# Two transformer layers with cross attention: cross keys in tiles of 512, 512, 450 and 127, the 450 first in a round, and small operations set between maxima

## The chip, the cores and the metric

The kernel runs on one core of a Trainium2 chip. The metric is the device time of one launch in microseconds, the median of several runs. TensorE (PE in the profile) multiplies matrices into PSUM, which has 8 banks of 128 partitions by 512 floats; VectorE (DVE), ScalarE (ACT) and GpSimd (POOL) do the rest; SyncE (SP, its queue SPq) issues nearly all the transfers (DMA).

## The reference

Two layers over x (4 sequences of 512 tokens, 320 wide) and a context (4 x 1601 tokens, 192 wide), all in float32. The part that the change touches is the attention, 20 heads of 16:

```
h1 = _ln(x, n1_g, n1_b)
x = _attn(h1, h1, q1, k1, v1, o1_w, o1_b, heads) + x
h2 = _ln(x, n2_g, n2_b)
x = _attn(h2, context, q2, k2, v2, o2_w, o2_b, heads) + x
...
sim = jnp.einsum('bhid,bhjd->bhij', q, k) * scale
a = jax.nn.softmax(sim, axis=-1)
out = jnp.einsum('bhij,bhjd->bhid', a, v)
```

A gated feed-forward layer follows in each of the two layers. The softmax is taken with the maximum of each row subtracted.

## The kernel before

**Units.** Attention is cut into units: one sequence and a group of 4 of the 20 heads. A layer has 20 self units (512 keys, 4 chunks of 128 keys) and 20 cross units (1601 keys, 13 chunks), then 4 feed-forward units. The four heads of a unit lie in four row groups of 32 partitions, so that matmuls of four heads can run side by side on PE.

**A round.** A unit's main loop takes one chunk of 128 keys a round (`main`). For each head `score` issues three matmuls of 512 columns into a bank named st: two of keys times queries (the queries are split in a high and a low part), and one that adds the rows nrows, the negated maxima. ACT takes the exponential out of st into pr. One round later `values` multiplies pr by the values into a bank named av, which ACT copies (vo) and POOL adds up.

**Maxima ahead.** The maxima must be known before a unit starts, so each round also computes scores of the next unit with queries on the partitions, only for their maxima: matmuls into banks named sps, reduced by DVE into pm (line 1083), one maximum for each query tile, head and key tile. `max_pairs` builds two queues for a unit, one for heads 2 and 3 and one for heads 0 and 1. An entry is a key tile of 512 of one query tile for both heads. Cross keys are cut into 512, 512, 512 and a rest of 65; the rest of all four query tiles shares one bank (66 columns each, reduced at line 1105). That makes 13 entries in each queue and 13 rounds in a cross unit. In a round the scores of heads 0 and 1 stand beside maxima of heads 2 and 3, then scores of 2 and 3 beside maxima of 0 and 1; `round_of` puts the passes of the four row groups into common slots, five in a round. `give` decides whether a round gets an entry, and whether whole further rounds of maxima are put in when the next unit is behind.

**End of a unit's maxima.** Two rounds before the end of a unit (`c == u.nch - 3`) `max_reduce` (line 1123, cross units only) takes the maximum over key tiles, and `max_end` makes a high part (1131), a low part (1134) and a transpose (1139), all on DVE, one behind the other. Four transfers on SPq (line 1147) carry the result into nrows; between cross units they are an errand that is issued at the end of the next round.

**Banks.** `bank` gives out the PSUM bank that is expected to be free first. The expectation is kept by `busy` and `written` from assumed durations. The same expectation decides in `taken` whether DVE or ACT copies the projections of values and keys.

Of the kernel before, what the change touches and what calls it, by code (L numbers as in the profile page):

```python
# [23 lines left out]
P = 128  # L24
# [24 lines left out]
AHEAD = 10  # L49
GAP = 3  # L50

PARTS = [(0, 2 * HG), (2 * HG, H)]
# [23 lines left out]
def kernel(ctx: ExitStack, tc: tile.TileContext, x, context, ws, out):  # L76
# [977 lines left out]
    def max_pairs(u):  # L1054

        full = u.nkeys // 512
        rest = u.nkeys - full * 512
        ns = full + (1 if rest else 0)
# [4 lines left out]
        def full_two(heads, t, s):  # L1063
            pss = []

            def product(e):
                for j, ps in zip(heads, pss):
                    nc.tensor.matmul(  # L1068
                        ps,
                        lhsT=u.q[j * SLOT : (j + 1) * SLOT, e, t * P : (t + 1) * P],  # L1070
                        rhs=u.kT[j * SLOT : (j + 1) * SLOT, u.k0 + s * 512 : u.k0 + (s + 1) * 512],
                        start=(e == 0),
                        stop=(e == 1),
                    )

            if ns == 1:
                to = u.nm[:, :, 0, t]
            else:
                to = u.pm[:, t, :, s]

            def reduce():
                for j, ps in zip(heads, pss):
                    nc.vector.tensor_reduce(to[:, j : j + 1], ps, AX.X, ALU.max)  # L1083
                    busy("dve", 0.6, ps)

            return heads, [lambda e=e: product(e) for e in range(2)], reduce, pss, lambda: pss.extend(bank("sps") for _ in heads)

        def rest_two(heads):
            pss = []
            w = rest + rest % 2  # L1090

            def product(t):
                for e in range(2):
                    for j, ps in zip(heads, pss):
                        nc.tensor.matmul(  # L1095
                            ps[:, t * w : (t + 1) * w],
                            lhsT=u.q[j * SLOT : (j + 1) * SLOT, e, t * P : (t + 1) * P],
                            rhs=u.kT[j * SLOT : (j + 1) * SLOT, full * 512 : full * 512 + w],
                            start=(e == 0),
                            stop=(e == 1),  # L1100
                        )

            def reduce():
                for j, ps in zip(heads, pss):
                    nc.vector.tensor_reduce(
                        u.pm[:, :, j, full], ps[:, : NQ * w].rearrange("p (t w) -> p t w", w=w)[:, :, :rest], AX.X, ALU.max,
                    )
# [4 lines left out]
        pairs = [  # L1112
            deque([lambda heads=heads, t=t, s=s: full_two(heads, t, s)] for s in range(full) for t in range(NQ))
            for heads in ((2, 3), (0, 1))
        ]
        if rest:
            for q, heads in zip(pairs, ((2, 3), (0, 1))):
                q.append([lambda heads=heads: rest_two(heads)])
        return pairs

    def max_reduce(u):
        if u.pm is not None:
            nc.vector.tensor_reduce(
                u.nm[:, :, 0, :].rearrange("p j t -> p t j"), u.pm, AX.X, ALU.max,
            )
            busy("dve", 0.25)

    def max_end(u):

        top, high, low = (u.nm[:, :, i, :] for i in range(3))  # L1130
        nc.vector.tensor_reduce(
            high.bitcast(F32R), top.rearrange("p j (t o) -> p j t o", o=1), AX.X, ALU.max, negate=True
        )
        nc.vector.tensor_reduce(
            low, u.nm[:, :, 0:2, :].rearrange("p j e t -> p j t e"), AX.X, ALU.add, negate=True
        )
        turned = two.tile([P, SLOT], F32, tag="turned", name="turned")

        nc.vector.transpose(turned.rearrange("p (j c) -> p j c", j=HG), u.nm[:, :, 1:3, :].rearrange("p j e t -> p j (e t)"))
        busy("dve", 0.6)  # L1140
        slots = u.rows.bitcast(F32).rearrange("(g s) n -> s g n", s=DH)[0].rearrange("g (t r) -> g t r", t=NQ)

        def rows():
            for i in range(P // SLOT):
                part = slice(i * SLOT, (i + 1) * SLOT)
                queue = (nc.sync, nc.scalar, nc.gpsimd, nc.sync)[i] if start["on"] else nc.sync
                queue.dma_start(out=slots[:, :, part], in_=turned[part, :])

        if u.cross and u.before.cross:
            u.rows_of = rows  # L1150
            errands.appendleft((clock["round"] + 1, yes, rows))
        else:
            rows()

# [132 lines left out]
    def main(u, give, nxt):  # L1287
# [62 lines left out]
        for c in range(u.nch):  # L1350
# [4 lines left out]
            else:  # L1355
                products = []
                for odd in range(2):
                    if odd:
                        tick()
                    pair, rounds = give(2 * c + odd)  # L1360
# [19 lines left out]
            if not last and c == u.nch - 3:  # L1380
                max_reduce(nxt)
                max_end(nxt)
# [52 lines left out]
    def ff_main(u, give, nxt):  # L1435
        done = 0

        def beside(room, n):
# [6 lines left out]
            if done == u.steps - 1 and nxt is not None and nxt.kind != "ff":  # L1445
                max_reduce(nxt)
                max_end(nxt)
            steps(True)
            for _ in range(n - 1):
# [149 lines left out]
    def giver(u):  # L1599
# [15 lines left out]
        def give(h, alone=False):  # L1615
# [21 lines left out]
            while owed >= 1.0 and any(left(v) for v in ahead) and not (alone and rounds and rest > -4):  # L1637
# [9 lines left out]
                at_once(v)  # L1647
                rounds.append([f for q in v.pairs if q for f in q.popleft()])
# [6 lines left out]
            return [], rounds  # L1655

# [24 lines left out]
    for chain in ("proj", "proj", "values", None):  # L1681
        round_of(first.pairs[0].popleft() + first.pairs[1].popleft())
        if chain:
# [3 lines left out]
    run("values")  # L1687
    max_reduce(first)
    max_end(first)
    loads.extend(load_x(2))  # L1690
    for fs in (load_out(0, "o1_w"), load_x(3), load_cross(0)):
# [3 lines left out]
    for _ in range(2):  # L1695
        round_of(second.pairs[0].popleft() + second.pairs[1].popleft())
        run("values")
# [51 lines left out]
```

## Time and profile before

| | |
|---|---|
| median of 3 runs | 2946.09 us (2944.18 to 2946.61) |
| span of the profiled execution | 2948.5 us |
| mean granted TensorE clock | 0.993 |
| instructions | 84388 |
| maxima of 512 keys into pm | 1920, mean 681 ns |
| maxima of the rests | 160, mean 425 ns |
| transposes at the end of a unit's maxima | 80, 16.9 us busy |

The profile is of one execution. Times in a timeline are microseconds from the span's start: start, duration, engine, line, instruction, what it writes and reads, and how many instructions of that kind are merged in the row; in brackets how long the engine had been idle and what released it. PEld is PE's weight load. The list of waits gives waiter, what it waited for, total us, number of times and the longest. Matmuls of different row groups overlap, so their durations do not add up.

### The profile page before, as it was taken

What the parts mean: (1) busy time and instruction counts of PE and PEld (TensorE: products, weight loads), DVE (VectorE), ACT (ScalarE), POOL (GpSimd) and SP (SyncE); (2) the same over time, 40 slices, a digit from 0 to 9 for tenths busy, and PEclk for the clock granted to TensorE, in tenths of its full rate; (3) what the DMA queues carried; (4) which work ended last, traced back from release to release, by engine and by line L of the source; (5) the groups of instructions that cost most, each with busy time, mean ns of one, the idle gap of its engine ahead of it and who ended that gap; (6) DMA issues with size and microseconds to landing.
All of it is one profiled execution on the core that took longest, in us unless ns stands there. A gap on an engine that the chain in (4) does not pass through costs nothing.

```text
span 2948.5 us, 84388 instructions
## 1 busy us (share of the span) xinstructions
PE 2871.7 (97%) x35018; PEld 1513.0 (51%) x35018; DVE 2060.2 (70%) x4031; ACT 1890.3 (64%) x3754; POOL 1287.7 (44%) x1409
## 2 busy tenths in 40 slices
PE   8999999999999999999999999999999999999999
PEld 4555555555555554355554555555555555544554
DVE  7777888888888878323258678888888888873221
ACT  3867677887877878501138676778778788783000
POOL 3556345545545545211225563455455464451110
PEclk8999999999999999999999999999999999999999
DMA  4444224232232112200113342222221121222000
GB/s 106 107 124 101 69 67 108 52 89 59 50 93 68 47 50 62 83 18 11 42 40 89 100 101 68 64 62 54 54 65 47 50 72 45 58 53 78 20 22 14
DMA packets 186543, 188.70 MB, mean 64 GB/s; under 512 B 69668, under 2 KB 137264, under 8 KB 186160
## 3 DMA queue, kind: packets, MB, share of 16 engines
q1 hardware_dynamic: 185368, 182.11, 24.4%
q8 instruction: 276, 4.52, 0.6%
q10 hardware_dynamic: 760, 1.18, 0.2%
q14 instruction: 107, 0.88, 0.1%
q0 software_dynamic: 32, 0.00, 0.0%
HBM read 55.76 MB, written 29.36 MB: 29 GB/s over the span
## 4 chain that ended last, share of the span: by engine, by line
PE 81%; DVE 13%; ACT 1%; DMA 1%; issue 1%; POOL 1%; SPq 1%; POOLq 0%; ACTq 0%; DVEq 0%
PE av L1326 22%; PE st L1300 16%; PE fps L1411 10%; DVE pm L1083 8%; PE sps L1068 6%; PE yps L1518 6%; PE vps L1029 5%; PE ops L1226 3%; PE kps L965 3%; PE qkps L900 3%; DVE nmax L1083 3%; PE fps L1471 2%; PE qps L941 2%; PE sps L1095 1%; ACT pr L1310 1%
## 5 line engine op out<-in xcount | busy, mean ns | idle before, releaser
L1310 ACT ACTIVATE pr<-st 128x512 f32<-128x512 f32 (+1 forms) x2720 | 1404.4, 604 | 399.8 <-PE st L1300 364.9
L1083 DVE TENSOR_REDUCE pm<-sps 128x1 f32<-128x512 f32 x1920 | 1188.0, 681 | 147.7 <-PE sps L1068 139.0
L1346 POOL TENSOR_TENSOR o<-o,vo 128x512 f32<-128x512 f32 x576 | 739.2, 1283 | 960.8 <-ACT vo L1345 937.5
L1068 PE MATMUL sps<-kT,q 32*128 32x512 f32 x4800 | 867.5, 430 | 10.6 <-DMA q<-low 3.4
L1300 PE MATMUL st<-q,kT 32*128 32x512 f32 (+1 forms) x5120 | 782.4, 420 | 2.2 <-ACT low L916 1.7
L1326 PE MATMUL av<-pr,vals 128*32 128x512 f32 (+1 forms) x5440 | 736.8, 607 | 45.5 <-ACT pr L1310 10.0
L1300 PEld LDWEIGHTS st<-q,kT 32*128 32x128 f32 (+1 forms) x5120 | 417.2, 180 | 290.4 <-issue 120.4
L1300 PE MATMUL st<-nrows,ones 32*128 32x512 f32 (+1 forms) x2720 | 539.1, 399 | 9.4 <-DMA nrows<-turned 9.4
L1068 PEld LDWEIGHTS sps<-kT,q 32*128 32x128 f32 x4800 | 425.6, 184 | 91.1 <-ACT pr L1310 13.4
L1083 DVE TENSOR_REDUCE nmax<-sps 128x1 f32<-128x512 f32 x640 | 396.3, 681 | 103.6 <-PE sps L1068 96.0
L1345 ACT COPY vo<-av 128x512 f32<-128x512 f32 x576 | 354.1, 615 | 23.9 <-PE av L1326 20.1
L1482 ACT ACTIVATE gl<-fps,b 128x512 f32<-128x512 f32 x80 | 54.6, 687 | 414.4 <-PE fps L1471 303.2
L1411 PE MATMUL fps<-hT,w 128*128 128x512 f32 x640 | 283.0, 597 | 0.0
L1326 PEld LDWEIGHTS av<-pr,vals 128*32 128x32 f32 (+1 forms) x5440 | 111.1, 108 | 320.4 <-DVE pm L1083 182.1
L1300 PEld LDWEIGHTS st<-nrows,ones 32*128 32x128 f32 (+1 forms) x2720 | 245.1, 180 | 34.4 <-issue 8.4
L1483 DVE SCALAR_TENSOR_TENSOR hid<-fps,b,gl 128x512 f32<-128x512 f32 x80 | 59.6, 748 | 241.1 <-ACT gl L1482 239.1
L1411 PEld LDWEIGHTS fps<-hT,w 128*128 128x128 f32 x640 | 119.3, 190 | 155.3 <-issue 152.1
L1518 PE MATMUL yps<-w,hid 128*128 128x320 f32 x640 | 176.3, 435 | 0.1
L1518 PEld LDWEIGHTS yps<-w,hid 128*128 128x128 f32 x640 | 120.4, 190 | 56.5 <-ACT gl L1482 4.5
L1226 PEld LDWEIGHTS ops<-wo,aT 112*32 112x32 f32 (+1 forms) x3072 | 97.9, 110 | 57.9 <-issue 41.2
L1226 PE MATMUL ops<-wo,aT 112*32 112x160 f32 (+1 forms) x3072 | 124.1, 300 | 0.7 <-POOL aT L1208 0.6
L517 POOL TENSOR_SCALAR root<-root 128x4 f32<-128x4 f32 x22 | 5.2, 237 | 263.9 <-DVE root L511 263.2
(91 smaller groups left out, 2493.1 us busy)
## 6 DMA issues: line engine op xcount, KB each, us to landing
kT<-stages SPq DMA_DIRECT2D x160, 200.2 KB
oway<-o SPq DMA_DIRECT2D x80, 256.0 KB
q<-high SPq DMA_DIRECT2D x160, 64.0 KB
q<-low SPq DMA_DIRECT2D x160, 64.0 KB
kT<-high SPq DMA_DIRECT2D x60, 128.0 KB
q<-high SPq DMA_DIRECT2D x60, 128.0 KB
kT<-low SPq DMA_DIRECT2D x57, 128.0 KB
aT<-oway SPq DMA_DIRECT2D x32, 224.0 KB
```

The source lines that it names most:

```text
L900: nc.tensor.matmul(ps[f : f + m, :w], lhsT=wqk[:n, k, f // GD, column : column + m], rhs=first.hT[:n, k, at : at + w], start=(k == 0), sto ...
L1029: nc.tensor.matmul(ps[f : f + m, :w], lhsT=u.kvT[:n, k, at + f : at + f + m], rhs=wv[:n, k, h0 * DH : h1 * DH], start=(k == 0), stop=(k == ...
L1068: nc.tensor.matmul(ps, lhsT=u.q[j * SLOT : (j + 1) * SLOT, e, t * P : (t + 1) * P], rhs=u.kT[j * SLOT : (j + 1) * SLOT, u.k0 + s * 512 : u ...
L1083: nc.vector.tensor_reduce(to[:, j : j + 1], ps, AX.X, ALU.max)
L1226: nc.tensor.matmul(ps[f : f + m, : D // 2], lhsT=aT[:n, k, f * NQ + t * SLOT : f * NQ + t * SLOT + m], rhs=wo[:n, k, cols], start=(k == 0) ...
L1300: nc.tensor.matmul(own[0][:r, :], lhsT=ones[rows, :r] if e == 2 else u.keys(rows, c), rhs=u.rows[rows, :] if e == 2 else u.q[rows, e, :], ...
L1310: nc.scalar.activation(p[:r], own[0][:r], AF.Exp)
L1326: nc.tensor.matmul(ps[j * SLOT : (j + 1) * SLOT, :], lhsT=columns_of[:r, head : head + SLOT], rhs=pr.pop((c, j))[:r, :], start=True, stop= ...
L1345: nc.scalar.copy(vo, ps)
L1346: nc.gpsimd.tensor_tensor(u.o, u.o, vo, ALU.add)
L1411: nc.tensor.matmul(ps, lhsT=w1[:, k, i * FF + c * P : i * FF + (c + 1) * P], rhs=natural(u.hT[:, k]), start=start, stop=stop,)
L1518: nc.tensor.matmul(ps[:, :D], lhsT=hid[c][:, t * P : (t + 1) * P], rhs=w2[:, c, :], start=(c == 0), stop=(c == NHC - 1),)
```

## The change

Cross keys are cut into 512, 512, 450 and 127. The number of entries stays 13 in each queue. A tile is now built for one head at a time (`one_tile`), and an entry joins two: in eight entries of each queue one tile of 450 of one head stands ahead of one of 512 of the other, in four both are 512, and the last holds the rests, now 4 x 127 keys of 128 columns. In the first eight entries those with a 450 alternate between the two queues. A round puts the half whose entry has a 450 first. The small operations that end a unit's maxima go into a list, and one of them is issued behind each maximum (`one_between`); what is left at the end of the round is issued there (`all_between`). The costs that `busy` is told follow the tile's width, and the rest's goes from 0.38 to 0.6.

```
+NARROW = 450
...
+        spans = [(at, min(512, u.nkeys - at)) for at in range(0, u.nkeys, 512)]
+        if u.cross:
+            spans = [(0, 512), (512, 512), (1024, NARROW), (1024 + NARROW, u.nkeys - 1024 - NARROW)]
...
+            def reduce():
+                nc.vector.tensor_reduce(to, own[0][:, :w], AX.X, ALU.max)
+                busy("dve", 0.065 + w * 0.00104, *own)
+                one_between()
...
-                    busy("dve", 0.38, ps)
+                    busy("dve", 0.6, ps)
+                    one_between()
...
+        for first, (a, b) in enumerate(((2, 3), (0, 1))):
+            wide = {j: deque((j, t, s) for s in range(2) for t in range(NQ)) for j in (a, b)}
+            slim = {j: deque((j, t, 2) for t in range(NQ)) for j in (a, b)}
...
+                if i == 12:
+                    q.append((False, [lambda a=a, b=b: rest_tiles((a, b))]))
+                elif i % 2 == first or i > 7:
+                    j, k = ((a, b), (b, a))[turn % 2]
+                    turn += 1
+                    q.append((True, entry(slim[j].popleft(), wide[k].popleft())))
+                else:
+                    q.append((False, entry(wide[a].popleft(), wide[b].popleft())))
...
+    def one_between():
+        if between:
+            between.popleft()()
...
+        between.extend(([over_spans] if u.pm is not None else []) + [leading, trailing, turn])
...
-                    products += [lambda j=j: score(c, j) for j in ((2, 3) if odd else (0, 1))] + pair
-                round_of(products)
+                    halves.append((not slim, [lambda j=j: score(c, j) for j in ((2, 3) if odd else (0, 1))] + pair))
+                round_of([f for _, half in sorted(halves, key=lambda h: h[0]) for f in half])
             u.scored = c + 1
 
             if extra and u.cross:
                 round_of(extra[0])
+            all_between()
             flush()
...
             if not last and c == u.nch - 3:
-                max_reduce(nxt)
                 max_end(nxt)
```

The first place is on PE, the last-but-one round of a cross unit: kT_135 and q_104 are that unit's keys and queries, kT_101 and q_103 those of the unit after the next, whose first maxima stand in this round. Before:

```order
L1300 MATMUL st<-q_104,kT_135 128x512 x2
L1068 MATMUL sps<-kT_101,q_103 128x512 x2
L1300 MATMUL st<-q_104,kT_135 128x512 x2
L1068 MATMUL sps<-kT_101,q_103 128x512 x2
L1300 MATMUL st<-nrows_97,ones 128x512 x2
L1300 MATMUL st<-q_104,kT_135 128x512 x4
L1068 MATMUL sps<-kT_101,q_103 128x512 x2
L1300 MATMUL st<-nrows_97,ones 128x512 x2
L1068 MATMUL sps<-kT_101,q_103 128x512 x2
```

And now:

```order
L1341 MATMUL st<-q_104,kT_135 128x512 x2
L1073 MATMUL sps<-kT_101,q_103 128x450
L1073 MATMUL sps<-kT_101,q_103 128x512
L1341 MATMUL st<-q_104,kT_135 128x512 x2
L1073 MATMUL sps<-kT_101,q_103 128x450
L1073 MATMUL sps<-kT_101,q_103 128x512
L1341 MATMUL st<-nrows_97,ones 128x512 x2
L1341 MATMUL st<-q_104,kT_135 128x512 x4
L1073 MATMUL sps<-kT_101,q_103 128x512 x2
L1341 MATMUL st<-nrows_97,ones 128x512 x2
L1073 MATMUL sps<-kT_101,q_103 128x512 x2
```

The number and place of the matmuls is the same; the first tile that is complete, and whose maximum DVE takes first, has 450 columns.

The second place is on DVE, the end of a cross unit's maxima: the rests (128x4), a further round of maxima, the small operations into nmax_95 and turned, and maxima of the unit after it. Before:

```order
L1105 TENSOR_REDUCE pm<-sps 128x4 x4
L1083 TENSOR_REDUCE pm<-sps 128x1 x4
L1123 TENSOR_REDUCE nmax_95<-pm 128x4x4
L1131 TENSOR_REDUCE nmax_95<-nmax_95 128x4x4
L1134 TENSOR_REDUCE nmax_95<-nmax_95 128x4x4
L1139 STREAM_TRANSPOSE turned<-nmax_95 128x32
L1083 TENSOR_REDUCE pm<-sps 128x1 x8
```

And now:

```order
L1109 TENSOR_REDUCE pm<-sps 128x4 x4
L1084 TENSOR_REDUCE pm<-sps 128x1 x5
L1160 TENSOR_REDUCE nmax_95<-pm 128x4x4
L1084 TENSOR_REDUCE pm<-sps 128x1
L1166 TENSOR_REDUCE nmax_95<-nmax_95 128x4x4
L1084 TENSOR_REDUCE pm<-sps 128x1
L1172 TENSOR_REDUCE nmax_95<-nmax_95 128x4x4
L1084 TENSOR_REDUCE pm<-sps 128x1
L1178 STREAM_TRANSPOSE turned<-nmax_95 128x32
L1084 TENSOR_REDUCE pm<-sps 128x1 x4
```

The transpose moved behind the fourth maximum of the next round. The four transfers of its result keep their place among SPq's instructions between cross units; in nine self units they moved behind one load of weights or inputs.

More of the change, by code (lines that the diff above doesn't have):

```diff
@@ L1116, in max_pairs, with entry @@
[L1116 to L1122, printed above, removed]
+        def entry(*tiles):
+            return [lambda x=x: one_tile(*x) for x in tiles]
+        if not u.cross:
+            return [
+                deque((False, entry((a, t, 0), (b, t, 0))) for t in range(NQ))
+                for a, b in ((2, 3), (0, 1))
+            ]
+        out = []
@@ L1123, in max_reduce, with all_between, max_end, over_spans @@
+        return out
+    between = deque()
+    def one_between():
+        if between:
+            between.popleft()()
+    def all_between():
+        while between:
+            between.popleft()()
+    def max_end(u):
+        top, high, low = (u.nm[:, :, i, :] for i in range(3))
+        turned = two.tile([P, SLOT], F32, tag="turned", name="turned")
+        def over_spans():
             nc.vector.tensor_reduce(
@@ L1126, in max_reduce @@
             busy("dve", 0.25)
[L1128 to L1153, printed above, removed]
@@ L1647, in give @@
                 at_once(v)
-                rounds.append([f for q in v.pairs if q for f in q.popleft()])
+                rounds.append([f for q in v.pairs if q for f in q.popleft()[1]])
                 owed -= 1.0
@@ L1687 @@
     run("values")
-    max_reduce(first)
     max_end(first)
+    all_between()
     loads.extend(load_x(2))
```

91 lines of the change are left out of this document (54 added, 37 removed).

## The prediction

> **What bounds the kernel now.** I read the page first, for how busy TensorE (PE) is and what the chain that ended last is made of.
>
> ```profile
> PE 2871.7 (97%) x35018; PEld 1513.0 (51%) x35018; DVE 2060.2 (70%) x4031; ACT 1890.3 (64%) x3754; POOL 1287.7 (44%) x1409
> ...
> PE 81%; DVE 13%; ACT 1%; DMA 1%; issue 1%; POOL 1%; SPq 1%; POOLq 0%; ACTq 0%; DVEq 0%
> ```
>
> PE carries the end, VectorE (DVE) stands in for it in 13% of the span. The list of waits (waiter <- waited for: total us, times, longest) says where:
>
> ```profile
> PEld av L1326 <- DVE pm L1083: 182.1, 370, 1.1
> ...
> PEld st L1300 <- ACT pr L1310: 103.1, 142, 0.8
> ...
> PEld st L1300 <- DVE pm L1083: 30.8, 78, 0.8
> ...
> PEld sps L1068 <- DVE pm L1083: 14.1, 42, 0.5
> ...
> PE st L1300 <- DMA nrows<-turned: 9.4, 9, 2.4
> ```
>
> The commonest is the weight load of av waiting for a maximum of a cross unit: av takes the PSUM bank that the maximum frees. The last row, nine waits for the rows of negated maxima, matters further down. Third, the timeline of one round (start, duration, engine, instruction, count):
>
> ```profile
> 611.05 0.50 PE L1300 MATMUL st<-q,kT 32*128 32x512 f32 x2
> ...
> 611.39 0.39 PE L1068 MATMUL sps<-kT,q 32*128 32x512 f32 x1
> ...
> 611.62 0.39 PE L1300 MATMUL st<-nrows,ones 32*128 32x512 f32 x2
> ...
> 611.83 2.48 DVE L1083 TENSOR_REDUCE pm<-sps 128x1 f32<-128x512 f32 x4 [0.36 <-PE sps L1068]
> ...
> 612.08 0.39 PE L1068 MATMUL sps<-kT,q 32*128 32x512 f32 x2
> ...
> 612.58 1.06 PE L1326 MATMUL av<-pr,vals 128*32 128x512 f32 x8
> 613.46 0.62 PE L1029 MATMUL vps<-wv,ctxT 96*32 96x128 f32 x16
> ...
> 614.01 0.50 PE L1300 MATMUL st<-q,kT 32*128 32x512 f32 x2
> ```
>
> Matmuls of the four row groups go side by side, one slot each 0.23 us (611.39 to 612.08 is three slots). The last slot starts at 612.08, so av could start near 612.31. It starts at 612.58: the first maximum begins at 611.83, lasts 0.68 and frees its bank at 612.51. About 0.2 us of PE is lost here, and the round's start, first tile, first maximum, av, projection, next start are one chain.
>
> **Narrow tile first.** Prices by form (count | busy us, mean ns):
>
> ```profile
> L1083 DVE TENSOR_REDUCE pm<-sps 128x1 f32<-128x512 f32 x1920 | 1188.0, 681 | 147.7 <-PE sps L1068 139.0 <-PE st L1300 4.5
> ...
> L1105 DVE TENSOR_REDUCE pm<-sps 128x4 f32<-128x260 f32 x160 | 61.2, 425 | 28.8 <-PE sps L1095 25.1
> ...
> L1068 PE MATMUL sps<-kT,q 32*128 32x512 f32 x4800 | 867.5, 430 | 10.6 <-DMA q<-low 3.4
> ...
> L1095 PE MATMUL sps<-kT,q 32*128 32x66 f32 x1280 | 75.2, 270 | 0.0
> ```
>
> DVE pays (681-425)/252 = 1.02 ns an element, so 62 keys fewer are 63 ns; a matmul's duration falls by (430-270)/446 = 0.36 ns a column, so the tile is there 22 ns sooner. The first maximum frees its bank 0.085 us earlier, less than the 0.2 us that PE idles, so all of it counts. It counts where the next round's start does not wait for ScalarE (ACT) instead: 370 waits less the 142 of st on ACT leave 228. In the order of the changed kernel the 450 stands first in the rounds with pairs 0 to 11. The last of a unit's 13 rounds gives its gain back where the next step finds the rows late, so 228 x 12/13 x 0.085 = **-18 us**. Bounds: the 63 ns alone give -13; all 370 waits at 0.085 give -31.
>
> The waits for maxima inside a round (78 and 42 times, 45 us) shrink by 63 ns where a narrow one stands ahead: 120 x 0.063 = 7.6; part of them stand behind copies and small operations, which stay. I take half, **-4** (0 to -8).
>
> **The rest tile.** Four maxima of 508 elements instead of 260, 4 x 0.25 = 1.0 us more per cross unit, and 16 tiles of 450 pay 16 x 0.063 = 1.0 back in the twelve other rounds: DVE's total stays. With DVE at 70% the heavier round is mostly covered by DVE's idle time; if that cover were gone in each of 40 units it would be 40 us. I take **+2** (0 to +8) outside the ends of units, where it is counted next. Columns of a head and query tile on PE stay 1602; matmuls and loads stay the same in number; the 10 copies that the planner moves from ACT to DVE are 0.36 us each and go into idle time, 0.
>
> **Small operations between the maxima.** The end of a unit's maxima, DVE and SyncE's queue (SPq), and where PE uses the rows (nrows) in the next unit:
>
> ```profile
> 799.91 1.65 DVE L1105 TENSOR_REDUCE pm<-sps 128x4 f32<-128x260 f32 x4 [0.61 <-PE sps L1095]
> 801.90 2.48 DVE L1083 TENSOR_REDUCE pm<-sps 128x1 f32<-128x512 f32 x4 [0.33 <-PE sps L1068]
> 804.30 0.21 DVE L1123 TENSOR_REDUCE nmax<-pm 128x16 f32<-128x64 f32 x1
> 804.54 0.17 DVE L1131 TENSOR_REDUCE nmax<-nmax 128x16 fp32r<-128x16 f32 x1
> 804.75 0.19 DVE L1134 TENSOR_REDUCE nmax<-nmax 128x16 f32<-128x32 f32 x1
> 804.97 0.21 DVE L1139 STREAM_TRANSPOSE turned<-nmax 128x32 f32<-128x32 f32 x1
> 805.11 4.92 DVE L1083 TENSOR_REDUCE pm<-sps 128x1 f32<-128x512 f32 x8
> ...
> 805.25 2.63 SPq L1147 DMA_DIRECT2D nrows<-turned  x4
> ...
> 810.29 0.40 PE L1300 MATMUL st<-nrows,ones 32*128 32x512 f32 x2
> ```
>
> How long the last row transfer takes to land is seen where PE waited for it, 1.19 us after the last issue (847.33 + 2.67 = 850.00, use at 851.19):
>
> ```profile
> 847.33 2.67 SPq L1147 DMA_DIRECT2D nrows<-turned  x4
> ...
> 851.19 0.49 PE L1300 MATMUL st<-nrows,ones 32*128 32x512 f32 x2 [0.61 <-DMA nrows<-turned]
> ```
>
> So the margin at 810.29 is 810.29 - 805.25 - 2.63 - 1.19 = 1.2 us. Now the transpose comes behind four maxima instead of ahead of them, and with it the four transfers, which keep their place on SPq. Maxima in a row are 0.60 apart ((2.48-0.68)/3); a small operation between them costs its duration less an overlap of about 0.08 (the next maximum starts at 805.11, the transpose ends at 805.18), so 0.13, 0.09 and 0.11 ahead of the transpose, 0.33. Chain at this end: four rest maxima now 0.60 apart from 799.91, to 802.31; four maxima, the first narrow, 2.34, to 804.65; four more with three small operations, 2.67, to 807.32; transpose 0.21; 0.07 to the first issue; 2.63; 1.19: landed at 811.42. PE asks at 810.29: a wait of 1.13.
>
> Two more ends, with less and with more room:
>
> ```profile
> 890.39 0.21 DVE L1139 STREAM_TRANSPOSE turned<-nmax 128x32 f32<-128x32 f32 x1
> ...
> 890.66 2.64 SPq L1147 DMA_DIRECT2D nrows<-turned  x4
> ...
> 889.87 0.39 PE L1300 MATMUL st<-nrows,ones 32*128 32x512 f32 x2
> ...
> 897.10 0.39 PE L1300 MATMUL st<-nrows,ones 32*128 32x512 f32 x2
> ```
>
> ```profile
> 935.57 0.21 DVE L1139 STREAM_TRANSPOSE turned<-nmax 128x32 f32<-128x32 f32 x1
> 935.87 2.48 DVE L1083 TENSOR_REDUCE pm<-sps 128x1 f32<-128x512 f32 x4
> ...
> 935.85 2.68 SPq L1147 DMA_DIRECT2D nrows<-turned  x4
> ...
> 942.06 0.39 PE L1300 MATMUL st<-nrows,ones 32*128 32x512 f32 x2
> ```
>
> A round's first maximum starts 0.21 after its first nrows matmul (611.62, 611.83). At the second end that is 890.08; plus 2.67, 0.21, 0.06, 2.64 and 1.19 gives 896.85, 0.25 before 897.10: no wait. At the third, 935.87 plus 2.67, 0.21, 0.07, 2.68, 1.19 is 942.69 against 942.06: 0.63. The mean is 0.59. In the new order 34 of the 40 cross units end this way (the others have no maxima left to stand between), 34 x 0.59 = 20. Where it waits (two of three, some 23), av's idle 0.2 in that round is gone anyway, since the maximum runs on meanwhile: 23 x 0.2, 4 to 5 less. Self units have three small operations and three maxima ahead of the transpose, and mostly more room; I take an estimate of 2 for them; in nine of them the four transfers now also stand behind one load on SPq, 2.63/4 = 0.66 us, which runs while they wait for the transpose. Together **+18**. Bounds: 0 if PE comes later than today for other reasons, +35 if all 34 are like the first.
>
> [...] The rows at 804.97 and 805.11 show the next one starting before the recorded end of the last; I keep 0.08 of overlap.
>
> What the lump costs today, 804.30 to 805.11, was the hope: the round's first maximum ends sooner. But at 890.39 and 935.57 it lies largely in DVE time ahead of the round's first tile, and where it delays av the time is taken back by the late rows, in whose chain it is counted. Behind the rows on SPq wait the moves of later keys; they are needed rounds later, 0 (to +3).
>
> **Sum.** -18 - 4 + 2 + 18 = -2 us. Against the profiled execution: 2948.5 to 2946.5; the measured median lies 2.4 lower, at 2946.09, so **2944**. A measurement of this kernel tells 0.2%, 5.9 us, from no change.
>
> **Rivals.** *The rows come in time.* If the next unit's first round reaches its nrows matmul about a microsecond later than I read it, or the transfers land sooner, only -18 - 4 + 2 = -20 is left: 2926. For it: today only 9 waits for these rows show; against it: at the first end the transpose is done at 807.53 instead of 805.18, and 2.35 is more than the margin of 1.2.
>
> *The rows decide (slower).* One mechanism: at every end the chain rest maxima, extra maxima, maxima with small operations runs without a gap on DVE, as at 799.91, so all 34 wait 1.13: 34 x (1.13 - 0.2) = 32 instead of 18, total +12: 2958. It breaks even at a mean wait of 0.8 and costs over 0.2% from about 0.96. For it: the rest tile's extra time lies right ahead of the end; against: the second end has no backlog.
>
> [...]
>
> *The change does not do what it says:* av's bank is not the narrow tile's, since the planner's costs changed too. Then only 18 + 2 is left: 2966.
>
> **Numbers.** Forecast 0.42 (2938 to 2949), rows in time 0.30, rows decide 0.16, rest matmuls 0.06, other bank 0.06. Faster by over 0.2% (below 2940.2): the second and a quarter of the first, 0.40; slower (above 2952): the last three, 0.28, and a little of the first, 0.29; within: 0.31. Range 2921 to 2962: from the second case with the wider bounds of the gain to the fourth and third; outside stay the other bank and the tails, under 0.2.
>
> **What would show it.** Right: waits of av on pm maxima shorter by some 0.08 each; typical rounds 2.96 become 2.88; a new row of PE st waiting on nrows <- turned with 15 to 25 us over 20 to 30 times, the transpose 2 to 3 us later against its round. Wrong: rows waits under 8 us (second case) or over 30 (third); the rest matmuls' slots longer than before; waits of av on pm as long as today.

## The result and the profile after

The changed kernel took 2967.02 us (median of 4 runs, 2964.68 to 2972.48), the kernel before, beside it, 2946.35 (2944.18 to 2948.6): a ratio of 1.0073, 95% interval 1.0059 to 1.0086. It is slower by 21 us, where the prediction had 2944 and a range of 2921 to 2962.

The profiled execution has a span of 2970.7 us (clock 0.990). Its engine times, and the chain that ended last by engine:

```profile
PE 2888.4 (97%) x35018; PEld 1538.4 (52%) x35018; DVE 2046.5 (69%) x4041; ACT 1885.0 (63%) x3744; POOL 1290.1 (43%) x1409
...
PE 84%; DVE 4%; DMA 3%; issue 2%; SPq 2%; POOL 2%; ACT 2%; POOLq 0%; ACTq 0%; DVEq 0%
```

DVE left the chain, 13% to 4%, which is what the change was to bring; DMA and SPq, 1% each before, stand in it with 5% together. The list of waits says which transfers:

```profile
PEld av L1367 <- DVE pm L1084: 156.9, 358, 0.7
...
PE st L1341 <- DMA nrows<-turned: 32.6, 35, 2.8
```

The waits of av for a maximum fell from 182.1 to 156.9 us; those of the score matmuls for the rows rose from 9.4 us over 9 times to 32.6 us over 35. The forms, for the prices:

```profile
L1084 DVE TENSOR_REDUCE pm<-sps 128x1 f32<-128x450 f32 x640 | 397.1, 621 | 157.3 <-PE sps L1073 152.7 <-PE st L1341 0.7
...
L1109 DVE TENSOR_REDUCE pm<-sps 128x4 f32<-128x508 f32 x160 | 98.9, 680 | 24.0 <-PE sps L1099 21.9 <-PE st L1341 2.0
L1099 PE MATMUL sps<-kT,q 32*128 32x128 f32 x1280 | 77.8, 273 | 0.0
```

The narrow maximum takes 621 ns, 60 less than one of 512 keys (681 before); 63 were worked out ahead. The timeline of the round that the prediction showed before (611.05 to 614.01, 2.96 us):

```profile
623.42 0.49 PE L1341 MATMUL st<-q,kT 32*128 32x512 f32 x2
...
624.20 2.42 DVE L1084 TENSOR_REDUCE pm<-sps 128x1 f32<-128x450 f32 x4 [0.35 <-PE sps L1073]
...
624.88 1.07 PE L1367 MATMUL av<-pr,vals 128*32 128x512 f32 x8
...
626.31 0.49 PE L1341 MATMUL st<-q,kT 32*128 32x512 f32 x2
```

It takes 2.89 us. DVE starts 0.78 us after the round does, exactly as before (611.83 - 611.05): the 22 ns that 62 columns fewer should have saved on PE do not show. av starts 1.46 after the round's start instead of 1.53. Over the second to ninth rounds of all cross units the medians say the same: the first maximum 0.78 us after the round's start in both executions, av 1.47 instead of 1.53.

The end of a unit's maxima, the one that the prediction worked out in full:

```profile
814.38 2.47 DVE L1109 TENSOR_REDUCE pm<-sps 128x4 f32<-128x508 f32 x4 [0.64 <-PE sps L1099]
...
816.77 2.94 DVE L1084 TENSOR_REDUCE pm<-sps 128x1 f32<-128x450 f32 x5
...
819.63 0.21 DVE L1160 TENSOR_REDUCE nmax<-pm 128x16 f32<-128x64 f32 x1
819.76 0.68 DVE L1084 TENSOR_REDUCE pm<-sps 128x1 f32<-128x512 f32 x1
820.35 0.16 DVE L1166 TENSOR_REDUCE nmax<-nmax 128x16 fp32r<-128x16 f32 x1
820.43 0.68 DVE L1084 TENSOR_REDUCE pm<-sps 128x1 f32<-128x512 f32 x1
821.03 0.17 DVE L1172 TENSOR_REDUCE nmax<-nmax 128x16 f32<-128x32 f32 x1
821.12 0.68 DVE L1084 TENSOR_REDUCE pm<-sps 128x1 f32<-128x512 f32 x1
821.72 0.20 DVE L1178 STREAM_TRANSPOSE turned<-nmax 128x32 f32<-128x32 f32 x1
...
821.98 2.62 SPq L1186 DMA_DIRECT2D nrows<-turned  x4
...
825.81 0.49 PE L1341 MATMUL st<-nrows,ones 32*128 32x512 f32 x2 [0.67 <-DMA nrows<-turned]
```

Each small operation is hidden but for 0.13, 0.08 and 0.09 us (from its start to the next maximum's); the prediction had 0.13, 0.09 and 0.11. But the transpose stands behind the last of them, four transfers of 0.65 us each follow, and the last lands 1.21 us after its issue (821.98 + 2.62 = 824.60, use at 825.81): PE waits. In 24 of the 40 cross units the first use now lies 1.19 to 1.22 us behind the last issue, that is, at the landing; before, in 7.

**Where the 22 us lie.** The two executions have the same 680 rounds in the same order (80 units: 4 for each self unit, 13 for each cross unit). Taking each round from its first score matmul to that of the next, and the difference of the two executions summed by place, in us:

| after less before | |
|---|---|
| until the first round | +1.5 |
| first rounds of the 40 cross units | +22.6 |
| second to ninth rounds of the cross units | -10.6 |
| their last four | -1.5 |
| first rounds of the 40 self units | +6.4 |
| their other rounds | +3.7 |
| together | +22.1 |

The narrow tile's gain is there, in the middle rounds. What is lost is lost where a unit begins: 26 of the cross units' first rounds grew by 0.2 us or more, 0.88 on the mean.

### The profile page after: what moved, and what is told of

It is laid out like the page before. It is cut to its first block, busy times and chain, and to the rows that moved or that the text cites. A ratio compares the mean times of both kernels' runs of the same rounds, so it can differ in the third digit from the quotient of the medians.

```text
span 2970.7 us, 84400 instructions
## 1 busy us (share of the span) xinstructions
PE 2888.4 (97%) x35018; PEld 1538.4 (52%) x35018; DVE 2046.5 (69%) x4041; ACT 1885.0 (63%) x3744; POOL 1290.1 (43%) x1409
## 4 chain that ended last, share of the span: by engine, by line
PE 84%; DVE 4%; DMA 3%; issue 2%; SPq 2%; POOL 2%; ACT 2%; POOLq 0%; ACTq 0%; DVEq 0%
PE av L1367 21%; PE st L1341 19%; PE fps L1452 9%; PE sps L1073 9%; PE yps L1559 6%; PE vps L1032 5%; PE ops L1267 3%; PE qkps L903 3%; PE kps L968 3%; PE fps L1512 2%; DVE nmax L1084 2%; DMA nrows<-turned 2%; PE qps L944 2%; ACT pr L1351 1%; PE sps L1099 1%
## 5 line engine op out<-in xcount | busy, mean ns | idle before, releaser
L1084 DVE TENSOR_REDUCE pm<-sps 128x1 f32<-128x512 f32 (+1 forms) x1920 | 1158.4, 660 | 178.7 <-PE sps L1073 153.9
L1073 PE MATMUL sps<-kT,q 32*128 32x512 f32 (+1 forms) x4800 | 871.6, 423 | 11.1 <-DMA q<-low 3.4
L1341 PE MATMUL st<-q,kT 32*128 32x512 f32 (+1 forms) x5120 | 794.7, 423 | 4.6 <-ACT low L919 4.3
L1341 PE MATMUL st<-nrows,ones 32*128 32x512 f32 (+1 forms) x2720 | 560.9, 403 | 33.3 <-DMA nrows<-turned 32.6
L1341 PEld LDWEIGHTS st<-q,kT 32*128 32x128 f32 (+1 forms) x5120 | 438.9, 180 | 294.4 <-ACT pr L1351 109.8
L1084 DVE TENSOR_REDUCE nmax<-sps 128x1 f32<-128x512 f32 x640 | 404.7, 680 | 123.3 <-PE sps L1073 113.9
L1073 PEld LDWEIGHTS sps<-kT,q 32*128 32x128 f32 x4800 | 431.6, 184 | 78.4 <-ACT pr L1351 16.4
L1341 PEld LDWEIGHTS st<-nrows,ones 32*128 32x128 f32 (+1 forms) x2720 | 261.6, 180 | 59.1 <-issue 40.6
L1367 PEld LDWEIGHTS av<-pr,vals 128*32 128x32 f32 (+1 forms) x5440 | 111.4, 108 | 296.4 <-DVE pm L1084 156.9
```

The source lines that it names most:

```text
L1073: nc.tensor.matmul(own[0][:, :w], lhsT=u.q[j * SLOT : (j + 1) * SLOT, e, t * P : (t + 1) * P], rhs=u.kT[j * SLOT : (j + 1) * SLOT, u.k0 + ...
L1084: nc.vector.tensor_reduce(to, own[0][:, :w], AX.X, ALU.max)
L1341: nc.tensor.matmul(own[0][:r, :], lhsT=ones[rows, :r] if e == 2 else u.keys(rows, c), rhs=u.rows[rows, :] if e == 2 else u.q[rows, e, :], ...
L1367: nc.tensor.matmul(ps[j * SLOT : (j + 1) * SLOT, :], lhsT=columns_of[:r, head : head + SLOT], rhs=pr.pop((c, j))[:r, :], start=True, stop= ...
```

## The experiments

**Theory A**: the small operations, set one by one between maxima, bring the rows later than the next unit wants them; that alone is the loss, and the narrow tile is a gain. **Theory B**: the wide rest tile or the planner's costs took the gain. **Theory C**: the narrow tile gives nothing. e5 adds a **theory D**: shorter maxima pay wherever they stand. Each run was timed in 4 to 11 executions beside the kernel before.

### e1_lump: the small operations in a lump again

```
             if not last and c == u.nch - 3:
                 max_end(nxt)
+                all_between()
```

> The changed kernel, but the four small operations follow one another right behind the last maximum, as before the change; tiles of 512, 512, 450 and 127 and the 450 first are kept. Theory A (the small operations, one by one between maxima, bring the transposed rows two to three us later, and that costs all that was lost: 22.6 us in the first rounds of the cross units and 10.2 us in the self units of the profiled execution, against a gain of 12 to 13 us from the narrow tile): 2967 - 33 = 2934 us, from 2930 to 2938, and the waits of the score matmuls for rows fall from 32.6 us to under 12. Theory B (the wider rest tile, its matmuls or the planner's other costs take the gain away, late rows cost little): 2960 to 2967 us. Theory C (late rows cost what was lost, but the narrow tile gives nothing either): 2946 us, as before.

Measured: 2936.28 us (2933.59 to 2939.21), ratio 0.9966 (0.9953 to 0.9978). The same end, in the timeline of this run:

```profile
802.42 0.21 DVE L1160 TENSOR_REDUCE nmax<-pm 128x16 f32<-128x64 f32 x1
...
802.67 0.17 DVE L1166 TENSOR_REDUCE nmax<-nmax 128x16 fp32r<-128x16 f32 x1
802.87 0.19 DVE L1172 TENSOR_REDUCE nmax<-nmax 128x16 f32<-128x32 f32 x1
803.09 0.21 DVE L1178 STREAM_TRANSPOSE turned<-nmax 128x32 f32<-128x32 f32 x1
803.23 4.81 DVE L1084 TENSOR_REDUCE pm<-sps 128x1 f32<-128x450 f32 x8
803.37 2.62 SPq L1186 DMA_DIRECT2D nrows<-turned  x4
...
808.32 0.40 PE L1341 MATMUL st<-nrows,ones 32*128 32x512 f32 x2
```

The rows have 2.33 us from the last issue (805.99) to the use, and the wait for rows is back at its old size:

```profile
PE st L1341 <- DMA nrows<-turned: 7.8, 9, 2.5
```

Theory A, to within 2 us; B and C fall. The change without the spreading is 10 us faster than the kernel before; the spreading cost 31 us. What the spreading was to save is small: against this run, the last four rounds of the 40 cross units in the changed kernel are shorter by 3.1 us together, 0.08 an end.

### e2_spread_only: nothing but the spreading

```
-NARROW = 450
+NARROW = 512
...
-                    busy("dve", 0.6, ps)
+                    busy("dve", 0.38, ps)
...
-                    halves.append((not slim, [...
+                    halves.append((False, [...
```

> The kernel before with nothing but the small operations one by one between maxima: tiles of 512, 512, 512 and 65, no tile put first. Theory A: 2946 + 23 + 10 = 2979 us, from 2970 to 2985. Theory B: within 4 us of 2946. Theory C: 2967 us, since the spreading alone would then be the whole difference.

Measured: 2983.54 us (2983.3 to 2985.99), ratio 1.013 (1.0114 to 1.0145). Its waits:

```profile
PEld av L1367 <- DVE pm L1084: 184.2, 372, 1.1
...
PE st L1341 <- DMA nrows<-turned: 34.1, 35, 3.0
```

The rows are waited for as in the changed kernel, the maxima as in the kernel before. The loss is the spreading's alone: 37 us against the kernel before, where no narrow tile gives any of it back.

### e3_lump_cross and e4_lump_self: one kind of unit at a time

```
                 max_end(nxt)
+                if nxt.cross:          # e4: if not nxt.cross:
+                    all_between()
```

> The changed kernel, with the four small operations in one lump where they end the maxima of a cross unit and one by one where they end those of a self unit. Theory A: 2967 - 22.6 = 2944 us, from 2940 to 2949. If the late moves of keys and queries in the self units carry most of the loss instead: 2956 to 2962 us.

> The changed kernel, with the four small operations in one lump where they end the maxima of a self unit and one by one where they end those of a cross unit. Theory A: 2967 - 10 = 2957 us, from 2953 to 2961, so that this run and the one with the lump at cross units share the 33 us between them. If the self units' loss was chance of the order (one unit lost 4.8 us, another won 3.2): 2964 to 2970 us.

Measured: e3 2944.17 us (2941.2 to 2947.38), ratio 0.9994 (0.9986 to 1.0003); e4 2957.43 (2954.43 to 2962.4), 1.0038 (1.0025 to 1.0052). Against the lump everywhere, spreading costs 8 us at self units and 21 at cross units; together 29 of 31. It adds up, and it lies where it should: e4's first cross rounds are 24.5 us longer than e1's and its self rounds the same; e3's cross first rounds differ by 1.8, its self rounds by 8.0.

### e5_narrow_last: the narrow tile kept, but never first

```
-                    q.append((True, entry(slim[j].popleft(), wide[k].popleft())))
+                    q.append((True, entry(wide[k].popleft(), slim[j].popleft())))
...
-                    halves.append((not slim, [...
+                    halves.append((False, [...
```

(and the lump of e1)

> The kernel of the first run (small operations in a lump, all tiles of the change kept), but the tile of 450 keys is never the first of its block. If the narrow tile pays only as the first of a block, since only the first maximum frees the bank that av waits for (theory A): 2936 + 12 = 2948 us, from 2944 to 2951, and rounds in the middle of a unit go back to 2.96 us. If shorter maxima pay wherever they stand (theory D): 2934 to 2938 us.

Measured: 2949.6 us (2945.03 to 2958.69), ratio 1.0016 (1.0004 to 1.0028), 13 us above e1. The wait of av, in e5 and in e1:

```profile
PEld av L1367 <- DVE pm L1084: 182.7, 384, 0.7
```

```profile
PEld av L1367 <- DVE pm L1084: 163.4, 375, 0.6
```

So 450 keys pay only as the first tile (A; D falls). Over the second to ninth rounds of the cross units the median start of av is back at 1.53 us behind the round's start, where e1 has 1.47. The gain is 13 us by the medians, and 19 of the wait went. Part of the 13 is the granted clock: the executions of e5 range from 2945.0 us (clock 0.995) to 2958.7 (0.990), those of e1 from 2933.6 (0.995) to 2939.2 (0.993), and the two profiled ones, both at 0.995, are 11.7 us apart.

### e6_rest_65 and e10_rest_mid: the price of the wide rest tile

In e6:

```
-            at, n = spans[-1]
+            at, n = spans[-1][0], 65
```

In e10:

```
-            for i in range(13):
-                if i == 12:
+            for i in range(12):
+                if i == 6:
                     q.append((False, [lambda a=a, b=b: rest_tiles((a, b))]))
-                elif i % 2 == first or i > 7:
+                if i % 2 == first or i > 7:
```

(both with the lump of e1; e6 leaves 62 keys of every cross unit out of its maxima, so it prices the tile and is no kernel to use)

> The kernel of the first run, but the rest tile takes 65 of its 127 keys, so 62 keys of a cross unit are left out of its maxima: matmuls of 66 columns and maxima of 4 times 65 elements, as before the change. It prices the wide rest tile. By the sum (an estimate of 2 us, since its maxima take 256 ns more 160 times, mostly beside other work): 2934 us, from 2932 to 2936. If the wide rest tile holds PE up, 160 times 0.256 us on the path is 41 us, and a quarter of it 10 us: 2924 to 2929 us.

> The kernel of the first run (2936 us), but the rest tile is the seventh of a unit's 13 entries, where it was the last. The sixth run priced the wide rest tile at 5 to 6 us. If that price is paid because its maxima, 680 instead of 425 ns, are the last ahead of the small operations and the rows: 2931 to 2934 us. If it is paid wherever the tile stands: 2935 to 2938 us.

Measured: e6 2930.74 us (2929.66 to 2934.58), ratio 0.9952 (0.9939 to 0.9964); e10 2934.09 (2932.31 to 2938.71), 0.9958 (0.9946 to 0.9971). The rest tile costs 5.5 us, between what the two readings of e6 expected. Little of that is its matmuls: 271 ns at 66 columns in e6, by the group's row, and 273 at 128 columns in the changed kernel; the whole group is busy for 76.0 us in e6 and 77.8 in the changed kernel (78.1 in e1), some 2 us more:

```profile
L1099 PE MATMUL sps<-kT,q 32*128 32x66 f32 x1280 | 76.0, 271 | 0.0
```

What is left points to DVE: its maxima take 680 instead of 425 ns, and 5.5 us is about an eighth of the 41 us that 160 such differences make. In e10 the last four rounds of the cross units are 15.0 us shorter than in e1 and the middle rounds 14.7 longer. That suggests that the tile takes its price along and that its place ahead of the rows is not what makes it dear; but the entries behind it, with a 450 first among them, moved one place too, so the 15 us are not its price alone. The median of e10 lies between what its two readings expected, and e10 and e1 have overlapping intervals: how much the place adds stays open.

### e7_behind_first: all four behind the first maximum

```
-        between.extend(([over_spans] if u.pm is not None else []) + [leading, trailing, turn])
+        def together():
+            if u.pm is not None:
+                over_spans()
+            leading()
+            trailing()
+            turn()
+
+        between.append(together)
```

> The changed kernel, with all four small operations behind the first maximum of the next round, at cross and self units alike: the rows come about 0.7 us later than with the lump, not 2 to 3. Theory A, by the slack of every unit's rows in the first run's trace (0.7 us more lateness counts 6 us at the cross units and nothing at the self units; the first maxima behind the lump come earlier, 1 to 2 us less): 2936 + 5 = 2941 us, from 2938 to 2944. If it is not the lateness that costs but small operations between maxima: near 2967 us. If the lump ahead of the first maximum is what costs: below 2934 us.

Measured: 2944.11 us (2941.98 to 2950.34), ratio 0.9995 (0.9987 to 1.0004), just above A's range (2938 to 2944). The size nearly came out, the place did not: against e1, the first rounds of cross units are only 1.5 us longer, where 6 were expected; the last round of a cross unit, one behind the one with the small operations, is longer by 0.21 to 0.56 us in 15 units (5.5 us over all); and the self units, where nothing was expected, are 3.7 us longer. With 0.7 us the rows are nearly in time; why the round behind the lump pays instead stays open: that the lump delays three maxima of its own round, and these the next, is a reading that no run shows.

### e8_two_queues: rows by two queues

```
-                    queue = (nc.sync, nc.scalar, nc.gpsimd, nc.sync)[i] if start["on"] else nc.sync
+                    queue = (nc.sync, nc.scalar, nc.gpsimd, nc.sync)[i] if start["on"] else (nc.sync, nc.gpsimd)[i % 2]
```

(with the lump of e1)

> The kernel of the first run, but the four transfers of rows go to two queues, two to SyncE's and two to GpSimd's, where SyncE's took all four one after the other at about 0.65 us each. Theory A, taken the other way round: rows 1.3 us earlier, so the 7.8 us of score matmuls that still wait for rows go, and moves behind them come sooner too: 2928 us, from 2925 to 2932. If rows by GpSimd come no earlier, since it stands waiting for ScalarE's copies (its adds wait for them 938 us in all): 2936 to 2945 us.

Measured: 3018.59 us (3015.23 to 3024.25), ratio 1.025 (1.0236 to 1.0264), far off both. The same unit's end, DVE, SPq and POOL:

```profile
815.14 0.21 DVE L1178 STREAM_TRANSPOSE turned<-nmax 128x32 f32<-128x32 f32 x1
815.41 1.36 SPq L1186 DMA_DIRECT2D nrows<-turned  x2
...
817.11 1.29 POOL L1387 TENSOR_TENSOR o<-o,vo 128x512 f32<-128x512 f32 x1 [2.22 <-ACT vo L1386]
...
818.35 0.85 POOL L820 CAST stages<-stages 128x801 fp32r<-128x801 f32 x1
...
819.28 1.60 POOL L821 TENSOR_TENSOR stages<-stages 128x801 f32<-128x801 f32 x1
...
820.82 1.10 POOL L1186 DMA_DIRECT2D nrows<-turned  x2
...
824.40 0.80 PE L1341 MATMUL st<-nrows,ones 32*128 32x512 f32 x2 [3.86 <-issue]
```

SPq issued its two by 816.77. GpSimd's two stood in its order behind an add that waited for ACT, a cast and a subtraction, and ended at 821.92. The rows are used 2.48 us after that, where rows from SPq were used 1.19 to 1.22 after their last issue at 22 of the changed kernel's 35 waits for them. Whether GpSimd's transfers also land later is not shown: the 3.86 us that PE idles here are put down to issue. Against e1 the first rounds of cross units grew by 66.3 us, the second to ninth by 15.8 and the self units by 8.8. The expectation had priced GpSimd's order at no more than 9 us. As a test of theory A it was not planned, but it bears it out: here the small operations are in a lump, the rows are late, and most of the loss lies where a cross unit begins. What GpSimd's other work lost by the transfers was not taken apart.

### e9_self_rows_next and e11_lump_self_next: moves or rows at self units

```
-            if u.cross and u.before.cross:
+            if not start["on"] and (not u.cross or u.before.cross):
                 u.rows_of = rows
                 errands.appendleft((clock["round"] + 1, yes, rows))
```

(e9 on top of e3, e11 on top of e1)

> The kernel of the third run (lump at cross units, one by one at self units, 2944 us), but the four transfers of a self unit's rows are issued one tick later, so that at about half of the ends a move of keys or queries, or another transfer, goes to SyncE's queue ahead of them instead of standing behind rows that wait for the transpose. If the 8 us by which the third run stands above the first come from the moves held up behind the rows: 2938 to 2941 us. If they come from the rows themselves being late at self units: 2944 to 2949 us, since the rows are later still.

> The kernel of the first run, but rows of self units are issued one tick later, as in the run beside it. The slack at self units is 2.1 to 10.7 us from the last issue to the first use, of which 1.2 is the landing, so later rows cost nothing there, and the moves that now go first come up to 2.6 us earlier: 2932 to 2936 us. If rows at self units are on the path as well: 2938 to 2944 us.

Measured: e9 2950.64 us (2946.85 to 2954.4), ratio 1.0012 (1.0003 to 1.0021); e11 2944.43 (2942.51 to 2947.79), 0.9993 (0.9984 to 1.0002). Both are 6 to 8 us slower than the kernel that they stand on, and by 0.4 to 1.6 us slower than even the slower of their two expected ranges: rows at self units are on the path. But the moves are as well: from e3 to e9 the first rounds of self units grew by 15.2 us, and their other rounds shrank by 7.0. Rows and moves share one queue, and whichever goes first makes the other late. What the other order costs is seen at the dearest place of the changed kernel, a self unit's third round, in two stretches: up to the end of PE's stall, and on to the next round. Columns: stretch, its us, busy time of each engine (instructions), granted clock, DMA share, GB/s. Before:

```profile
199.26:201.95 2.69, 0.96 (x12) 0.49 (x11) 1.29 (x2) 0.53 (x2) 0.00 (x0) 1.00 0.64 126
201.95:206.69 4.74, 4.57 (x70) 2.80 (x70) 1.61 (x3) 3.68 (x8) 3.14 (x3) 1.00 0.18 56
```

And after:

```profile
203.52:208.80 5.28, 0.96 (x12) 0.49 (x11) 1.46 (x4) 0.53 (x2) 0.00 (x0) 0.90 0.74 181
208.80:215.78 6.98, 6.98 (x69) 3.81 (x69) 1.71 (x4) 3.81 (x8) 3.15 (x3) 0.58 0.12 38
```

And in e1, where the lump keeps the transpose early:

```profile
198.50:201.38 2.88, 0.97 (x13) 0.50 (x12) 1.29 (x2) 0.53 (x2) 0.00 (x0) 1.00 0.62 128
201.38:207.78 6.40, 6.23 (x69) 3.36 (x70) 1.61 (x3) 3.78 (x8) 3.16 (x3) 0.73 0.14 42
```

The two rounds ahead take 10.72 us before and after (188.54 to 199.26, 192.80 to 203.52). Then PE stands 2.59 us longer in the changed kernel than before (2.69 to 5.28) and 2.40 longer than in e1 (2.88). The rest of the round is 2.24 us longer than before (4.74 to 6.98), at a clock of 0.58; but e1, at 0.73, takes 6.40 for it. So of the 4.83 us that this round lost against the kernel before (7.43 to 12.26), 2.98 are the spreading's; the other 1.85 are lost in e1 too, most of them at its lower clock. What PE stands for, and the queue ahead of that, in the changed kernel:

```profile
187.57 0.20 DVE L1178 STREAM_TRANSPOSE turned<-nmax 128x32 f32<-128x32 f32 x1
187.84 2.67 SPq L1186 DMA_DIRECT2D nrows<-turned  x4
...
191.23 0.58 SPq L758 DMA_DIRECT2D ctxT<-stages  x1
197.20 5.25 SPq L772 DMA_DIRECT2D w<-ctxT  x8
202.54 0.54 SPq L869 DMA_DIRECT2D kT<-high  x1
...
208.28 0.84 ACT L919 ACTIVATE low<-qkps,scales 128x256 f32<-128x256 f32 x2 [6.94 <-DMA q<-low]
208.80 0.79 PE L1341 MATMUL st<-q,kT 32*128 32x512 f32 x2 [4.32 <-ACT low L919]
```

The queue in the kernel before, with the same load and moves:

```profile
184.23 0.58 SPq L755 DMA_DIRECT2D ctxT<-stages  x1
190.24 5.10 SPq L769 DMA_DIRECT2D w<-ctxT  x8
195.44 0.54 SPq L866 DMA_DIRECT2D kT<-high  x1
```

The rows wait for the transpose. The load behind them is issued 1.57 us ahead of the unit's start (191.23, 192.80), before it was 4.31 ahead (184.23, 188.54), 2.7 us sooner; the moves behind that come 9.74 us after the start (202.54), before 6.90 (195.44); ACT's next copy waits for the moves to have read its buffer (6.94 us of idle, 208.28), and PE for the copy (4.32 us, 208.80).

### e12_narrow_480

```
-NARROW = 450
+NARROW = 480
```

(with the lump of e1)

> The kernel of the first run with cross keys in tiles of 512, 512, 480 and 97 instead of 512, 512, 450 and 127. If gain and price both go with the number of keys taken from the first tile (32 of 62; 10 us between the kernel before and the first run): 2946 - 5 = 2941 us, from 2939 to 2943. If the first maximum is soon enough already with 480 keys: 2934 to 2938 us.

Measured: 2936.19 us (2935.15 to 2943.93), ratio 0.9967 (0.9954 to 0.9979): no difference from 450. That is in the range expected if 480 keys were soon enough already, but the trace speaks against that reading. The wait of av is up again (163.4 us in e1):

```profile
PEld av L1367 <- DVE pm L1084: 176.4, 387, 0.6
```

The middle rounds are 4.6 us longer than e1's, so the gain shrank by about half; the last four rounds of the cross units, where the rest stands, are 4.3 us shorter. Gain and price cancel between 450 and 480, and neither expectation had them move apart.

## Why the prediction was wrong

The mechanism was named and had the largest positive term; the step that failed is its size, **+18** for late rows, where the runs showed 31. All other sizes were off to the same side. By the medians (after is 20.7 us above before):

| step | predicted | measured | from |
|---|---|---|---|
| 450 first | -18 | -13 | e5 less e1 |
| shorter waits inside rounds | -4 | (-2) | not measured: what is left of the total |
| rest tile | +2 | +5.5 | e1 less e6 |
| spreading at cross units | +16 | +21 | e4 less e1 |
| spreading at self units | +2 | +8 | e3 less e1 |
| both kinds together | +18 | +31 | after less e1 |
| sum | -2 | +21 | |

**450 first.** "all of it counts" took 63 ns from DVE and 22 ns from PE. The 63 ns alone give -13, which the prediction wrote down as its bound; 13 came out by the medians, 11.7 between two executions at the same clock. The count of 228 rounds was not tested by itself. The 22 ns had been read off the durations of matmuls that run beside others. The durations did fall (407 ns with 450 columns, 429 with 512), but the first maximum starts 0.78 us after the round's start with 450 columns as with 512.

**Rest tile.** A mis-sized term inside its bounds (0 to +8). That the rest matmuls cost, to which the chances gave 0.06, no run shows beyond some 2 us: one takes 273 ns at 128 columns and 271 at 66 in e6, the whole group 77.8 us instead of 76.0.

**Rows late at cross units.** The step that failed most by weight is the choice of 18 between bounds of 0 and 35: 13 of the 23 us that the sum missed, 5 of them at cross units, 6 at self units, and 2 that show only when both are spread. The working at single ends was fair but not sharp: less the 0.2 us that av's idle gives back, 0.93, 0 and 0.43 us were worked out for the three ends, and their first rounds grew by 0.78, -0.06 and 1.28. Three ends were too few to stand for 34 or 40. And the prediction priced the waits alone, while the granted clock fell too: on the mean it is 0.9944 in the executions of e1 and 0.9915 in those of the changed kernel, which by an estimate (0.0029 of 2967 us) is 9 of the 31 us. No term stood for that.

**Rows late at self units.** "an estimate of 2" and, of the moves behind the rows, "they are needed rounds later, 0 (to +3)": both failed: 8 us were measured. The slack at self units was never listed, though the trace of before has it: from the last issue to the first use, less the landing of 1.2 us, it is 0.9 to 8.1 us over the 40 units, and nine of them have less than 2.2. In the changed kernel 28 of the 40 have less than 2.2. And moves needed rounds later are needed sooner by someone else: by ACT, whose next copy into the staging buffer stood idle until a move had read it, for 6.94 us at 208.28 in the changed kernel.

**The lump.** That it cost little today, and that the hope lay there, was right: 3.1 us over 40 cross units.

**The weighing.** The rival that ends slower, "the rows decide", was this mechanism with a larger mean, and got 0.16; its 2958 was short too, since it left the self units as they were. "Rows in time" got 0.30 on the strength of only 9 waits in the trace of before. That count says how often the margin is used up already, not how large it is elsewhere.

**The signs named ahead.** Waits of av shorter by 0.08 each and rounds of 2.88: av came 0.07 sooner in the round shown (1.53 to 1.46) and 0.06 by the medians, and the round took 2.89. Rows waits of 15 to 25 us meant the forecast, over 30 the rival; it was 32.6, over 35 times where 20 to 30 were forecast.

## What to carry to other kernels

A small operation at the head of a dependent chain (transpose, four transfers, a landing, the first matmul of the next unit) is worth its place ahead of larger work even if the engine then delays that work: here, at a cross unit, 0.08 us an end was saved by spreading and 0.5 paid (21 us over 40 ends), and at a self unit 0.2 (8 over 40). Before moving a step later, list the slack of its result at every use, not at two or three, and then ask what is queued behind its transfers. A change of several parts is worth taking apart: the new tiles alone, with the small operations left in a lump, ran at 2936 us (ratio 0.9966), faster than both kernels.

## What the runs showed of the hardware

- A lower clock followed some stalls. In the self unit above PE idled 4.32 us (5.28 less 0.96 busy), and the granted clock of the 6.98 us that followed was 0.58; the same rest of the round took 4.74 us before, at 1.00. A pair of score matmuls shows 0.79 us there, and 0.49 at 623.42. Over the whole, PE's idle time (span less busy) is 60.3 us in the execution of e1 and 82.3 in that of the changed kernel, 22.0 more, and the clock is 0.995 and 0.990; by an estimate (0.010 of 2970.7 us less 0.005 of 2932.5) that is 15 us more. Together they are 37 of the 38.2 us between the two executions.
- How long a stall has to be for that, and whether the stall is the cause, is not shown. The 4.32 us were followed by a clock of 0.58, the same unit's stall of before, 1.73 us (2.69 less 0.96), by 1.00. But in e1 a stall of 1.91 us (2.88 less 0.97) was followed by 0.73, and in the kernel before one of 1.53 us (1062.07 to 1063.60) by 0.58 over the next 8.1 us, while one of 2.36 us (1636.63 to 1638.99) was followed by 1.00 over the next 8.0. And from 1526 to 1529 the kernel before shows 0.50 with PE busy for all of it, and for 2.58 of the 3 us ahead.
- A transfer of rows (4 KB, four in a row on SPq) took 0.65 us to issue (2.62 for the four at 821.98). Where PE waited for the rows, it used them 1.19 to 1.21 us after the last issue at 7 of the 9 waits before the change (2.92 and 3.75 at the others), and 1.19 to 1.22 after it at 22 of the 35 in the changed kernel (1.11 to 3.83 at the others).
- In e8 the transfers that GpSimd issued stood in that engine's order of work. The group of these transfers (count, then busy us, mean ns, then the idle time just before them and what ended it) reads:

```profile
L1186 POOL DMA_DIRECT2D nrows<-turned x159 | 90.1, 568 | 118.0 <-PE sps L1073 49.9 <-DVE turned L1178 42.8 <-PE kps L968 15.4
```

  One takes 0.57 us, so it is not the length of the issue that made the rows late. It was its place behind other work, with GpSimd idle for 118 us ahead of such transfers, standing for what others had yet to do; at the end shown above the two were issued from 820.82 to 821.92, where SPq's were through by 816.77.
- DVE started the next maximum before the recorded end of a small operation, by 0.08 us at the end shown above: 819.63 + 0.21 is 819.84, and the next starts at 819.76; 820.51 against 820.43 and 821.20 against 821.12 say the same.
